# One exp over 1024 columns and a VectorE row sum for the score pair that TensorE masks, in the first batch of a two-layer graph network

## The chip, the cores and the metric

The kernel runs on one core of a Trainium2 chip. The core has five engines with a queue each, all working in parallel: TensorE (PE; its weight loads are listed apart as PEld), VectorE (DVE), ScalarE (ACT), GpSimd (POOL) and SyncE (SP), which here only issues DMAs. They share SBUF; TensorE writes its results to PSUM, from where VectorE and ScalarE read them. The metric is the device time of one execution in microseconds (us). Lower is better.

## The reference

Sixteen graphs of 1024 nodes with 256 features each go through two layers. Cut to what matters:

```
# layer 0, for each graph b: h is a relu of a layer norm of x
normed = layer_norm(h, gamma1, beta1)              # 8 heads of 32 columns; q = k = v
scores = einsum('bhqd,bhkd->bhqk', qkv, qkv) / sqrt(32)
masked = where(adj > 0, scores, -inf)
attn   = softmax(masked, axis=-1)                  # exp, and a sum over the keys
h      = h + einsum('bhqk,bhkd->bhqd', attn, qkv)
x      = x + h + gelu(layer_norm(h) @ W1 + b1) @ W2 + b2
# layer 1: a second attention over the same graph, with leaky relu, softmax and elu
```

The scores are symmetric, since queries and keys are the same, and so is the mask of these inputs. A sum over one axis therefore equals a sum over the other.

## The kernel before

The work of one graph (a "batch" b, 0 to 15) is split into streams: the attention of layer 0 (`attention`), its preparation (`prologue`: layer norms, values `va`, keys `kT`), the masks (`turn_masks`, `compare_masks`), and everything after the attention (`rest`: the two-layer perceptron and all of layer 1). The streams run as Python generators that are merged by a planned place in time; the attention of batch b + 1 is laid between the matmuls of the rest of batch b. Some instructions are put off by a planned number of microseconds (`defer`). What results is one fixed order of instructions for each engine, and at the end of `fast_path` a loop ties every instruction to the one before it on its engine, so that the order written is the order run.

The attention of a batch goes by units (qh, g, kt): a half of the queries (512), a group of four heads, and a tile of 128 keys. The first batch has 2 x 2 x 8 = 32 units, and nothing of a `rest` to lie between them. A unit does the following:

- `scores` (L978): TensorE multiplies keys by queries for four heads (L994) into two PSUM tiles of 128 x 2 x 512, `sc0` for heads 0 and 1 (pair 0) and `sc1` for heads 2 and 3 (pair 1). There is one buffer of each, so the next unit's matmuls into `sc0` wait until this unit's `sc0` has been read.
- The mask is a tile of 0 and of a large negative number. In the first batch (`by_pe = 2 if b == 0 else 0`, L984) TensorE adds it to pair 0 itself, by a matmul with the identity ahead of the scores (L988, its matmuls are listed under the helper's line L574). Pair 1 gets it from VectorE (L1007), which writes the masked scores to an SBUF tile `e`. In all later batches VectorE does this for both pairs.
- ScalarE takes the exponential, one head of 512 columns at a time, and adds up each row as it goes, into a column of a tile `sums`. This is the nested function `weights` (L1011); an exp with such a sum shows as two instructions, ACTIVATE and ACTIVATION_READ_ACCUMULATOR:

```
nc.scalar.activation(
    e[:, j], masked[:, j], AF.Exp, scale=SCALE,
    accum_out=sums[kt // TPH, g][:, n, kt % TPH, qh : qh + 1],
)
```

- For pair 0, `weights` is called inside the loop (L1019), ahead of pair 1's mask addition; for pair 1 it is returned and called by `attention` after the previous unit's `weigh` (L1104: the weights times the values, L1109).
- `invert` (L1125) adds up `sums` over the key halves and takes the reciprocal `rl`; `finish` (L953) turns the result by TensorE (`ptos`, L960), scales it (`ot`, L962) and lets GpSimd add it to `h` (L966).

The engines do other things during the first batch. `setup` multiplies weights (`p_wT`, `p_wb`, `p_wm`, `p_w_a`; copies L678, L694). The prologue of batch 1 takes layer norm statistics on VectorE (`st`, `mv` and `ve`, L741 to L744), their power on GpSimd (`rs`, L746), a factor `nm` on VectorE (L798), a relu on ScalarE (L803), then normalizes, multiplies and adds on GpSimd (`nrm` L750 and L816, `va` L817); TensorE turns `va` (`ptk`, L824) and ScalarE copies it to `kT` (L827). In the first batch's own prologue `nrm` is normalized by VectorE. Mask tiles are converted by VectorE (`mq`, L594), loaded and turned by DMAs of the SP queue (L587, L904), and compared for symmetry by GpSimd and VectorE (`odd` L919, `uneven` L926). At its end `rest` of batch 0 begins: `prepare` (statistics `st_c`), `y` (GpSimd), its turn `pty` (L1275), `yT` (VectorE, L1279), `ph` (TensorE).

Of the kernel before, what the change touches and what calls it, by code (L numbers as in the profile page):

```python
# [14 lines left out]
AF = mybir.ActivationFunctionType  # L15
ALU = mybir.AluOpType
# [479 lines left out]
def fast_path(  # L496
# [28 lines left out]
    nc = tc.nc  # L525
# [10 lines left out]
    TPH = QW // P  # L536
# [3 lines left out]
    SCALE = 1.0 / math.sqrt(HD)  # L540
# [28 lines left out]
    def matmul(out, lhsT, rhs, start=True, stop=True):  # L569
        if not quarters[0]:  # L570
            nc.tensor.matmul(out, lhsT, rhs, start=start, stop=stop)  # L571
            return
        for c in range(0, P, HD):
            nc.tensor.matmul(out[c : c + HD], lhsT[:, c : c + HD], rhs, start=start, stop=stop)  # L574
# [393 lines left out]
    def attention(b, st):  # L968
        va, kT = st["va"], st["kT"]
        mirrored = b > 0  # L970
        sums = {}
# [6 lines left out]
        def scores(qh, g, kt):  # L978
            qs = slice(qh * QW, (qh + 1) * QW)
            sc = [  # L980
                psc.tile([P, 2, QW], F32, tag=f"sc{i}", name=f"s_{b}_{g}_{qh}_{kt}_{i}") for i in range(2)
            ]

            by_pe = 2 if b == 0 else 0  # L984
            if by_pe:
                for j in range(by_pe):
                    matmul(
                        sc[j // 2][:, j % 2, :], ident8, st[qh][:, kt // 2, :, kt % 2], start=True, stop=False  # L988
                    )
                clock[0] += 0.45  # L990
            for j in range(GH):
                r = slice(j * HD, (j + 1) * HD)
                for c in range(0, P, P // 2):
                    nc.tensor.matmul(  # L994
                        sc[j // 2][c : c + P // 2, j % 2, :],
                        kT[r, g, kt * P + c : kt * P + c + P // 2],
                        kT[r, g, qs],
                        start=j >= by_pe,
                        stop=True,
                    )  # L1000
            mb = st[qh][:, kt // 2, :, kt % 2].unsqueeze(1).to_broadcast([P, 2, QW])
            es = []
            for i in range(2):
                e = ep.tile([P, 2, QW], F32, tag="e", name=f"e_{b}_{g}_{qh}_{kt}_{i}")
                masked = sc[i]
                if 2 * i >= by_pe:
                    nc.vector.tensor_tensor(e, masked, mb, op=ALU.add)  # L1007
                    masked = e
                es.append(e)

                def weights(e=e, masked=masked, i=i):  # L1011
                    for j in range(2):
                        n = 2 * i + j
                        nc.scalar.activation(  # L1014
                            e[:, j], masked[:, j], AF.Exp, scale=SCALE,
                            accum_out=sums[kt // TPH, g][:, n, kt % TPH, qh : qh + 1],
                        )

                if i == 0:  # L1019
                    weights()  # L1020
            return es, weights


# [126 lines left out]
        for n, u in enumerate(units):  # L1150
            qh, g, kt = u
            make_turns()
            es, rest_of_weights = scores(*u)
            go_on()
            rest_of_weights()
            first = n == 0 or units[n - 1][:2] != u[:2]
# [488 lines left out]
    while any(p is not None for p in places):  # L1645
        i = min((p, i) for i, p in enumerate(places) if p is not None)[1]
# [72 lines left out]
```

## Time and profile before

| what | value |
|---|---|
| median of three runs | 3445.18 us (3441.09 to 3447.68) |
| the profiled execution | 3447.03 us, its span 3445.2 us |
| TensorE busy over the span | 3250.0 us, 94% |
| VectorE | 2669.7 us, 77% |
| ScalarE | 1987.4 us, 58% |
| GpSimd | 1856.5 us, 54% |
| first exp of the first batch | starts at 23.64 us |
| the last unit's mask addition (unit 32) | starts at 142.19 us |
| L1014, first batch's pair 0 (`e<-s`): 64 exps | 590 ns each, and 64 accumulator reads of 198 ns |
| L1014, all others (`e<-e`): 1504 exps | 619 ns each, and 1504 reads of 187 ns |
| L1007, mask addition, 752 times | 1218 ns each |

How to read it: the profile is one execution, seen by the hardware. Instructions are grouped by line, engine, operation and tile. The idle time before an instruction is given with what ended it. Busy shares are averages over stages that have different limits; the first batch is about 4% of the span.

### The profile page before, as it was taken

What the parts mean: (1) busy time and instruction counts of PE and PEld (TensorE: products, weight loads), DVE (VectorE), ACT (ScalarE), POOL (GpSimd) and SP (SyncE); (2) the same over time, 40 slices, a digit from 0 to 9 for tenths busy, and PEclk for the clock granted to TensorE, in tenths of its full rate; (3) what the DMA queues carried; (4) which work ended last, traced back from release to release, by engine and by line L of the source; (5) the groups of instructions that cost most, each with busy time, mean ns of one, the idle gap of its engine ahead of it and who ended that gap; (6) DMA issues with size and microseconds to landing.
All of it is one profiled execution on the core that took longest, in us unless ns stands there. A gap on an engine that the chain in (4) does not pass through costs nothing. (4 is left out here: it accounts for less than half of the span.)

```text
span 3445.2 us, 114688 instructions
## 1 busy us (share of the span) xinstructions
PE 3250.0 (94%) x48866; PEld 1597.5 (46%) x48866; DVE 2669.7 (77%) x4889; ACT 1987.4 (58%) x4808; POOL 1856.5 (54%) x2006
## 2 busy tenths in 40 slices
PE   6899999999999999999999999999999999999998
PEld 2244444444444444444444444444444444444477
DVE  5678787887878778787887887878788787877744
ACT  6765755647456474655646556575564745646542
POOL 4664663645656465563656737466364565635230
PEclk9999999999999999999999999999999999999999
DMA  5255455464554544545454555545546455554510
GB/s 134 50 123 145 104 122 125 112 159 102 128 120 116 144 112 122 129 114 143 112 133 112 122 139 119 140 106 125 125 112 159 100 131 118 121 142 102 128 38 14
DMA packets 741159, 404.81 MB, mean 118 GB/s; under 512 B 173217, under 2 KB 699937, under 8 KB 740641
## 3 DMA queue, kind: packets, MB, share of 16 engines
q1 hardware_dynamic: 740352, 397.14, 47.7%
q8 instruction: 386, 6.32, 0.8%
q14 instruction: 133, 1.08, 0.1%
q10 hardware_dynamic: 288, 0.26, 0.0%
HBM read 233.97 MB, written 146.54 MB: 110 GB/s over the span
## 5 line engine op out<-in xcount | busy, mean ns | idle before, releaser
L1014 ACT ACTIVATE e<-e 128x512 f32<-128x512 f32 x1504 | 929.3, 619 | 829.5 <-DVE e L1007 827.4
L1007 DVE TENSOR_TENSOR e<-s,mk 128x1024 f32<-128x1024 f32 x752 | 885.9, 1218 | 219.2 <-PE s L994 212.4
L574 PE MATMUL ph<-yT,w 128*32 128x256 f32 x7808 | 445.7, 379 | 23.5 <-DVE yT L1279 15.9
L574 PE MATMUL lg<-fT,uT 128*32 128x256 f32 x7680 | 455.7, 381 | 0.0
L994 PE MATMUL s<-kT 32*64 32x512 f32 x6272 | 451.3, 627 | 1.2 <-DVE e L1007 1.2
L574 PE MATMUL pa<-gw,e 128*32 128x258 f32 x7584 | 446.4, 380 | 0.1
L574 PE MATMUL po<-w,hid 128*32 128x256 f32 x7680 | 442.6, 379 | 0.0
L1109 PE MATMUL o<-e,va 128*32 128x512 f32 x3136 | 432.8, 619 | 1.4 <-ACT e L1014 1.4
L574 PEld LDWEIGHTS ph<-yT,w 128*32 128x32 f32 x7808 | 250.6, 110 | 226.8 <-DVE yT L1279 32.3
L574 PEld LDWEIGHTS po<-w,hid 128*32 128x32 f32 x7680 | 249.9, 110 | 203.0 <-issue 48.8
L574 PEld LDWEIGHTS lg<-fT,uT 128*32 128x32 f32 x7680 | 249.2, 110 | 195.3 <-issue 22.5
L574 PEld LDWEIGHTS pa<-gw,e 128*32 128x32 f32 x7584 | 247.5, 110 | 185.3 <-issue 26.2
L966 POOL TENSOR_TENSOR h<-h,ot 128x512 f32<-128x512 f32 x64 | 84.4, 1319 | 455.7 <-DVE ot L962 455.7
L1030 DVE STREAM_TRANSPOSE x<-e 128x1024 f32<-128x1024 f32 x240 | 296.2, 1239 | 42.3 <-ACT e L1014 40.8
L1043 POOL TENSOR_TENSOR part<-part,x 128x512 f32<-128x512 f32 x240 | 316.7, 1320 | 18.8
L1397 DVE SCALAR_TENSOR_TENSOR e<-lg,gw,mk 128x256 f32<-128x256 f32 x512 | 223.0, 476 | 112.0 <-PE lg L574 100.7
L1014 ACT ACTIVATION_READ_ACCUMULATOR e<-e 128x1 f32 x1504 | 281.5, 187 | 0.0
L1403 ACT ACTIVATE e<-e,shift 128x512 f32<-128x512 f32 x256 | 183.1, 716 | 158.4 <-DVE e L1402 150.5
L1303 ACT ACTIVATE hid<-ph,b1c 128x256 f32<-128x256 f32 x512 | 202.8, 466 | 83.4 <-PE ph L574 63.9
L1043 POOL TENSOR_TENSOR part<-x 128x512 f32<-128x512 f32 x120 | 155.4, 1295 | 176.2 <-DVE x L1030 114.7
L919 POOL TENSOR_TENSOR odd<-mk,mq 128x512 bf16<-128x512 fp8e5 x192 | 234.0, 1226 | 18.1 <-DVE uneven L926 15.6
L746 POOL TENSOR_TENSOR rs_c<-ve_c,mhalf 128x2 f32<-128x2 f32 x64 | 45.6, 713 | 359.4 <-DVE ve_c L744 323.9
(144 smaller groups left out, 4613.7 us busy)
## 6 DMA issues: line engine op xcount, KB each, us to landing
blocks<-x SPq DMA_DIRECT2D x480, 256.0 KB, 4.7
em<-blocks SPq DMA_DIRECT2D x240, 512.0 KB, 5.0
adj<-in_adj_dram SPq DMA_DIRECT2D x248, 256.0 KB, 3.9
h<-in_x_dram SPq DMA_DIRECT2D x64, 256.0 KB, 4.1
xb<-in_x_dram SPq DMA_DIRECT2D x128, 128.0 KB, 3.3
out_dram<-z SPq DMA_DIRECT2D x128, 128.0 KB, 3.9
rows<-row SPq DMA_DIRECT2D x120, 32.0 KB, 2.3
gather<-rows SPq DMA_DIRECT2D x120, 32.0 KB, 3.4
```

What stands on the lines that cost most here:

```text
L574: nc.tensor.matmul(out[c : c + HD], lhsT[:, c : c + HD], rhs, start=start, stop=stop)
L919: nc.gpsimd.tensor_tensor(odd.rearrange("p (u v x) -> p u v x", u=2, v=2), key.rearrange("p (u v x) -> p u v x", u=2, v=2), query.rearrang ...
L966: nc.gpsimd.tensor_add(ho, ho, ot.rearrange("p t j d -> p t (j d)"))
L994: nc.tensor.matmul(sc[j // 2][c : c + P // 2, j % 2, :], kT[r, g, kt * P + c : kt * P + c + P // 2], kT[r, g, qs], start=j >= by_pe, stop= ...
L1007: nc.vector.tensor_tensor(e, masked, mb, op=ALU.add)
L1014: nc.scalar.activation(e[:, j], masked[:, j], AF.Exp, scale=SCALE, accum_out=sums[kt // TPH, g][:, n, kt % TPH, qh : qh + 1],)
L1030: nc.vector.transpose(x[:, :, 2 * i : 2 * i + 2, :].rearrange("p c h j -> p h c j"), es[i].rearrange("p h (c i) -> p h c i", i=HD),)
L1043: add = lambda out, p, q: nc.gpsimd.tensor_tensor(out, p, q, op=ALU.add)
L1109: nc.tensor.matmul(o[j * HD : (j + 1) * HD, :], va[:, kt, (g * GH + j) * HD : (g * GH + j + 1) * HD], es[j // 2][:, j % 2, :], start=first ...
L1303: nc.scalar.activation(hid[:, f0 + i, :], ph[:, i, :], AF.Identity, bias=b1c[:, f0 + i : f0 + i + 1])
L1397: nc.vector.scalar_tensor_tensor(e[:, j, :], lg[:, j, :], gw[:, kt, D : D + 1], st[c // 2][:, kt // 2, qs, kt % 2], op0=ALU.add, op1=ALU.add,)
L1403: ready = defer(2.5, lambda: nc.scalar.activation(e, e, AF.Exp, bias=shift))
```

## The change

For the pair whose mask TensorE adds (pair 0, in the first batch only), `weights` issues a single exp over both heads, 1024 columns, without a row sum. VectorE then adds up each head's 512 results by a `tensor_reduce` over `e`, into the two columns of `sums`. The call for pair 0 is moved behind the loop, so that both instructions come after pair 1's mask addition on VectorE's queue. Nothing changes for pair 1, or for the later batches.

```diff
                 def weights(e=e, masked=masked, i=i):
+                    if 2 * i < by_pe:
+                        nc.scalar.activation(e, masked, AF.Exp, scale=SCALE)
+                        nc.vector.tensor_reduce(
+                            sums[kt // TPH, g][:, 2 * i : 2 * i + 2, kt % TPH, qh : qh + 1].rearrange(
+                                "p h o -> p (h o)"
+                            ),
+                            e, axis=mybir.AxisListType.X, op=ALU.add,
+                        )
+                        return
                     for j in range(2):
                         n = 2 * i + j
                         nc.scalar.activation(
...
-                if i == 0:
+                if i == 0 and by_pe == 0:
                     weights()
+                elif i == 0:
+                    first = weights
+            if by_pe:
+                first()
             return es, weights
```

## The prediction

> **What bounds the kernel now.** The change touches only the first batch (`by_pe` is 2 for b = 0 and 0 for all others), so I read the page for the whole and then only the first 146 us. The page gives PE 94% of the span. From 146 us on, where the next stage joins the first attention's successor, PE has almost no gaps, so a delay of the first batch's end is carried to the end of the kernel unchanged. The question is thus when the 32 units of the first batch are done. First the waits of 20 to 146 us (who waited for whom, us in total, times, longest):
>
> ```profile
> PE s L574 <- ACT e L1014: 10.0, 18, 1.4
> ...
> PE ptk L824 <- POOL va L817: 6.4, 3, 2.9
> ```
>
> TensorE waits for the first pair's exps before it can write the next unit's masks, 18 times; and three times for GpSimd, which prepares the next batch's values. Then the timeline of one quiet unit (start, duration, engine; the bracket is the idle time before it):
>
> ```profile
> 42.25 0.60 ACT L1014 ACTIVATE e<-s 128x512 f32<-128x512 f32 x1 [0.39 <-PE s L994]
> 42.34 1.22 DVE L1007 TENSOR_TENSOR e<-s,mk 128x1024 f32<-128x1024 f32 x1 [1.52 <-ACT e L1014]
> ...
> 43.32 0.20 ACT L1014 ACTIVATION_READ_ACCUMULATOR e<-s 128x1 f32 x1
> ...
> 43.57 0.61 PE L574 MATMUL s<-mk,ident 128*32 128x512 fp8e5 x8 [0.42 <-ACT e L1014]
> ...
> 43.60 0.63 ACT L1014 ACTIVATE e<-e 128x512 f32<-128x512 f32 x1
> ```
>
> The reader is to see a ring: exps of pair 0 from 42.25 to 43.52, which free `sc0`; masks from 43.57; scores from 44.12; the next exp at 45.33. A turn takes 3.08 us, of which PE idles 0.42 and VectorE (DVE) about 1.5. Such slack is not everywhere. In other units DVE goes from one add to the next without a gap:
>
> ```profile
> 68.41 1.23 DVE L1007 TENSOR_TENSOR e<-s,mk 128x1024 f32<-128x1024 f32 x1 [3.04 <-PE s L994]
> 69.55 0.75 DVE L594 TENSOR_SCALAR mq<-adj 128x512 fp8e5<-128x512 int32 x2
> 70.22 0.42 DVE L741 BATCH_NORM_STATS2 st_b<-h 128x6 f32<-128x256 f32 x1
> ...
> 71.50 1.22 DVE L1007 TENSOR_TENSOR e<-s,mk 128x1024 f32<-128x1024 f32 x1
> ```
>
> Last the busy times by stretch (length, then PE, PEld, DVE, ACT, POOL):
>
> ```profile
> 58.95:83.90 24.95, 20.01 (x312) 5.83 (x312) 17.09 (x44) 21.50 (x66) 8.87 (x12) 1.00 0.43 112
> 83.90:113.50 29.60, 22.59 (x236) 6.13 (x220) 16.59 (x28) 20.98 (x65) 28.63 (x30) 0.96 0.00 1
> ```
>
> DVE is two thirds busy in the first; GpSimd has 28.63 of 29.60 us in the second and is the bound there. Its run starts with one DVE result, and PE stands at its end:
>
> ```profile
> 83.90 0.69 POOL L746 TENSOR_TENSOR rs_a<-ve_a,mhalf 128x2 f32<-128x2 f32 x1 [2.36 <-DVE ve_a L744]
> ```
> ```profile
> 112.67 0.90 PE L824 MATMUL ptk<-ident,va 128*128 128x128 f32 x3 [2.48 <-POOL va L817]
> ```
>
> [...] The trace agrees: the copies from PSUM of 257 and 512 columns take 353 and 564 ns, 0.827 a column. [...] The two rows below agree: 391 ns for 386 columns more, 1.01 a column. [...]
>
> ```profile
> L728 DVE TENSOR_REDUCE seen<-sq 128x1 f32<-128x512 f32 x1 | 0.7, 675 | 0.0
> ...
> L1230 DVE TENSOR_REDUCE seen<-good 128x1 f32<-128x126 f32 x1 | 0.3, 284 | 0.0
> ```
>
> **Prices.** Exp over 1024 columns from PSUM: 590 ns for 512 (row L1014 e<-s) + 512 x 0.83 = 1.02 us. It frees `sc0` 1.02 us after its start, where the two exps and their accumulator reads took 1.27: 0.25 less a turn. On ACT's queue the two took 1.14 us from start to start of what follows (75.04 to 76.18 us), the one takes about 0.92. Bounds: 0.96 and 1.10. The reduce: [...] 1.21 us, like the add of as many columns (1.22), whose follower starts 1.14 after it; so 1.13 us more of DVE's queue a unit. Bounds: [...] 1.35 (two reduces of 512).
>
> **Part by part.** Removed: 64 exps of 512 and their 64 accumulator reads on ACT. Added: 32 exps and 32 reduces, 32 x 1.13 = 36 us of DVE. Moved: the exp is issued after the add, on another engine, so ACT's order stays. The reduce waits for its exp; behind it in DVE's queue stand the layer norm statistics (GpSimd's `rs` waits for them), `nm` (ACT's relu L803 waits for it), the mask conversions (SP's DMAs wait for these) and the next add. The exp usually ends before the add does (42.25 + 1.02 against 43.48), so that wait costs nothing unless ACT is late. No DMA is added, and PE's list is the same.
>
> Now the units in order, by the lag of the new against the old (minus is earlier):
> - Units 1 to 5 (23.7 to 39.3 us). The reduce stands ahead of the statistics on which GpSimd's `rs_b`, the `nrm` of DVE and so the next add depend (25.4 to 33.15 us, GpSimd without a gap from 27.5). All move by 1.13: **+1.13**.
> - Units 5 to 11. Four turns have PE waiting for ACT: 4 x -0.25. The two others are full of other PE work (`p_wT`, `p_wb`): 0. DVE needs 1.14 + 1.13 + 0.34 = 2.61 us of the new 2.83 in the quiet ones. Lag **+0.13**; the add of unit 10 is at +0.25 for its mask conversion.
> - Unit 11 to 12: DVE 1.14 + 1.13 + 1.27 of statistics = 3.54 against 3.09. Add at +0.59. Unit 13 starts behind exp, relu and the copy of `wm` (63.4 to 66.0), all behind that add: +0.6.
> - 13 to 14: 1.14 + 1.13 + 0.67 + 1.28 = 4.22 against 3.09: +1.7. 14 to 15: 3.62 against 3.07: +2.3. 15 to 16: DVE has nothing else, back to +1.45. 16 to 17: 3.61 against 3.07: +2.0.
> - Unit 17: relu L803 waits for `nm`, now at 83.2 for 80.6; the exp behind it starts at 84.36, the reduce at 84.36 + 1.05 = 85.41; then 1.13 and 1.26 of statistics: `ve_a` at 87.80 for 83.65. Lag **+4.15**.
> - GpSimd's run of 83.9 to 112.6 starts by so much later and has no room; DVE's and PE's lags in it, up to 5, are covered by it. At 113.5: +4.15.
> - Units 25 to 32: two quiet turns give -0.5. At 128.75 the mask conversions come behind a reduce and `rl` behind both: +0.3. The DMAs of the masks, released by those conversions, land later by 4.8 (before: conversions waiting for them at 132.93, 133.63 and 138.06), and adds 30 and 31 with them: +4.8. The last reduce stands beside the wait for `pty`.
>
> Sum: **+4.8 us** at 146 us, and to the end. The profiled execution took 3447.03 us (span 3445.2), so 3451.8 against it; it lay 1.85 above the median of 3445.18, so I predict **3450.0 us**. The bounds of the reduce move the sum by about -1 and +2 (13 units where DVE is the bound), those of the exp by about 0.5, my reading of which wait ends last by 3 to 4.
>
> **Rivals.**
> - *B, the second pair's exps wait for the reduce.* Reduce and exps write columns of the same tile `sums`. If that is taken as a conflict, ACT's second pair starts after the reduce, 2.5 us after the first exp instead of 1.35; a turn is 2.5 + 1.25 = 3.75 us for 3.08. That is some 0.9 worse than the forecast in the six turns bound by ACT or PE before 60 us, 1.1 at each of units 12, 14 and 16, and 3 after 113 us: about +15, 3460. Against it: the columns are disjoint (heads 0, 1 and 2, 3). It decides as soon as the wait exists. This is the case on the other side.
> - *C, DVE's backlog outlasts the first batch.* Its add of unit 32 is at +5.3; if `yT` at 145.34, on which `ph` waits, comes behind more of such work, PE loses another 3 to 5: 3454. For it: after 200 us DVE is 90% busy and more.
> - *D, hidden.* The statistics ahead of 83.9 are not the last arrival; the run of GpSimd starts as before: about 0, 3445. Against it: GpSimd idled 2.36 us for exactly that.
> - *E, the ring decides.* All 18 waits of PE shrink by 0.25: -4.5, 3440.7. The most that 32 units could give is 8 us.
>
> **How the numbers follow.** 0.2%, 6.9 us, is about what a measurement of this kernel can tell from no change. Forecast 0.52, own range 3445 to 3455 (0.34 of it within 0.2%, 0.18 above), B 0.12, C 0.14, D 0.13, E 0.09 (0.05 beyond 0.2%, and 0.01 of D). Slower 0.18 + 0.12 + 0.14 = 0.44, same 0.50, faster 0.06. The range from 3443 to 3460 leaves E's side and B's upper side out.
>
> **What would show it.** L1014 e<-s 32 times near 1.02 us, the reduce 32 times near 1.21, quiet turns of 2.83 us, `ve_a` near 88 and `va` near 117 us. B would show as ACT's e<-e waiting for the reduce. Wrong I am if GpSimd's run starts near 84, or if PE makes up the lag after 146 us.

## The result, and the profile after

The changed kernel takes 3457.8 us (median of 8 runs, 3452.47 to 3464.07) and the kernel before, measured beside it, 3445.1 us (8 runs, 3440.16 to 3450.47). The ratio is 1.0036, with a 95% interval from 1.0025 to 1.0046: by the ratio 12.4 us slower, with 8.6 to 15.8 as the interval. The profiled execution took 3458.48 us, its span 3456.6 us. The forecast was 3450.0 with a range to 3460: the side is right, and the loss is more than twice the 4.8 us of the forecast.

I read the trace in the order of the prediction. First the two new groups, from the list of groups by shape, 20 to 160 us of the changed kernel (busy us and mean ns of one; then the idle time before them):

```profile
L1014 DVE TENSOR_REDUCE sum<-e 128x2 f32<-128x1024 f32 x32 | 38.8, 1211 | 2.6 <-ACT e L1013 2.6
L1013 ACT ACTIVATE e<-s 128x1024 f32<-128x1024 f32 x32 | 32.6, 1019 | 13.4 <-PE s L994 13.3
```

Both prices are the predicted ones, 1.21 and 1.02 us. A quiet turn is the predicted one too (2.83 us for 3.08): ScalarE's timeline of the changed kernel has the wide exp 2.84 us after the last, and nothing stands between the wide exp and pair 1's but the mask addition.

```profile
43.24 1.02 ACT L1013 ACTIVATE e<-s 128x1024 f32<-128x1024 f32 x1 [0.20 <-PE s L994]
44.54 0.63 ACT L1023 ACTIVATE e<-e 128x512 f32<-128x512 f32 x1 [0.27 <-DVE e L1007]
...
46.08 1.03 ACT L1013 ACTIVATE e<-s 128x1024 f32<-128x1024 f32 x1 [0.20 <-PE s L994]
```

So the single prices hold, and the sum does not. The waits of the changed kernel, 20 to 160 us, say where (us in total, times, longest):

```profile
PE s L574 <- ACT e L1013: 9.0, 15, 2.5
...
PE ptk L824 <- POOL va L817: 6.9, 3, 3.3
POOL odd L919 <- DVE uneven L926: 6.7, 3, 3.3
```

TensorE's waits for the exps went from 10.0 us in 18 waits to 9.0 us in 15; that is all that is left here of the shorter turns. The third line is the news: GpSimd waits three times for VectorE's `uneven`, where before it did so once, for 2.37 us at 40.90. Two of the three lie in its full run, of which I had said that it covers VectorE's lag. GpSimd's timeline of the changed kernel:

```profile
89.48 0.69 POOL L746 TENSOR_TENSOR rs_a<-ve_a,mhalf 128x2 f32<-128x2 f32 x1 [3.92 <-DVE ve_a L744]
...
98.88 1.15 POOL L919 TENSOR_TENSOR odd<-mk,mq 128x512 bf16<-128x512 fp8e5 x1
102.49 1.16 POOL L919 TENSOR_TENSOR odd<-mk,mq 128x512 bf16<-128x512 fp8e5 x1 [2.46 <-DVE uneven L926]
...
114.78 1.16 POOL L919 TENSOR_TENSOR odd<-mk,mq 128x512 bf16<-128x512 fp8e5 x1 [0.98 <-DVE uneven L926]
...
121.18 0.72 POOL L817 TENSOR_TENSOR va<-nrm,be 128x256 f32<-128x256 f32 x1
```

The run begins 5.58 us late (83.90 before), loses 2.46 and 0.98 us inside, and its last `va` starts 9.29 us late (111.89 before). TensorE stands at its end, as before, and the lag goes on from there (TensorE's timeline of the changed kernel, then of the kernel before: the masks of unit 25):

```profile
121.96 0.90 PE L824 MATMUL ptk<-ident,va 128*128 128x128 f32 x3 [2.65 <-POOL va L817]
122.79 1.04 PE L574 MATMUL s<-mk,ident 128*32 128x512 fp8e5 x8
```
```profile
113.50 1.04 PE L574 MATMUL s<-mk,ident 128*32 128x512 fp8e5 x8
```

The first scores of the second batch start at 154.75 us for 145.23, +9.52. In the later batches of this profile the lag moves between 7 and 12 us, and at the end of the span it is 11.4. A second profile of the changed kernel has the same lag at the second batch, counted from the first mask addition, and only 2.4 us at the end of its span, so a single profile does not tell what is left at the end; the two timed ratios, 1.0036 and 1.0037, do. Why GpSimd had to wait is in VectorE's timeline of the changed kernel around the first of the two waits:

```profile
98.18 1.21 DVE L1007 TENSOR_TENSOR e<-s,mk 128x1024 f32<-128x1024 f32 x1
100.86 1.22 DVE L1014 TENSOR_REDUCE sum<-e 128x2 f32<-128x1024 f32 x1 [1.47 <-ACT e L1013]
102.00 1.93 DVE L926 TENSOR_TENSOR uneven<-uneven,odd 128x256 int32<-128x256 int32 x2
```

A comparison goes through two buffers of `odd`: GpSimd writes one, VectorE adds it to `uneven` and so frees it. From 98.88 to 100.03 GpSimd filled the second; the addition that would free the first stood behind the new reduce, and the reduce waited 1.47 us for its exp. The third comparison began only after 102.00.

### The profile page after: what moved, and what is told of

The parts are those of the page before. It is cut to its first block, busy times and chain, and to the rows that moved or that the text cites. A ratio compares the mean times of both kernels' runs of the same rounds, so it can differ in the third digit from the quotient of the medians.

```text
span 3456.6 us, 114602 instructions
## 1 busy us (share of the span) xinstructions
PE 3259.9 (94%) x48866; PEld 1598.3 (46%) x48866; DVE 2704.1 (78%) x4921; ACT 1985.6 (57%) x4712; POOL 1861.4 (54%) x2006
## 3 DMA queue, kind: packets, MB, share of 16 engines
q14 instruction: 132, 1.08, 0.1%
## 5 line engine op out<-in xcount | busy, mean ns | idle before, releaser
L1007 DVE TENSOR_TENSOR e<-s,mk 128x1024 f32<-128x1024 f32 x752 | 885.6, 1218 | 199.9 <-PE s L994 194.8
L994 PE MATMUL s<-kT 32*64 32x512 f32 x6272 | 458.7, 633 | 3.4 <-DVE e L1007 3.4
```

The lines of the kernel that those rows point to most:

```text
L994: nc.tensor.matmul(sc[j // 2][c : c + P // 2, j % 2, :], kT[r, g, kt * P + c : kt * P + c + P // 2], kT[r, g, qs], start=j >= by_pe, stop= ...
```

## The experiments

Marks are counted from the first mask addition of VectorE, since that start itself lies between 23.70 and 24.66 us from profile to profile. They are the addition of unit 11, the start of GpSimd's full run (`rs_a`), the masks of unit 25 on TensorE (the end of that run), and the first scores of batch 2 (the end of the first batch). Ratios are against the kernel before, timed beside each on the same chip.

| kernel | unit 11 | run | unit 25 | batch 2 | median us | ratio, 95% interval |
|---|---|---|---|---|---|---|
| before | 35.30 | 60.17 | 89.77 | 121.50 | 3445.1 | 1 |
| changed | 36.52 | 65.78 | 99.09 | 131.05 | 3457.8 | 1.0036 [1.0025, 1.0046] |
| a_again (the changed kernel once more) | 36.58 | 65.79 | 99.09 | 131.06 | 3451.94 | 1.0037 [1.0021, 1.0052] |
| e1_short | 34.38 | 59.50 | 89.47 | 120.23 | 3443.65 | 0.9991 [0.9982, 1.0000] |
| e7_reduce_only | 39.33 | 70.00 | 102.35 | 133.13 | 3460.03 | 1.0043 [1.0028, 1.0057] |
| e2_odd_own | 38.91 | 68.77 | 98.28 | 130.65 | 3453.57 | 1.0023 [1.0015, 1.0031] |
| e2_again | 38.37 | 67.70 | 97.23 | 129.01 | 3453.94 | 1.0020 [1.0011, 1.0029] |
| e4_late_reduce | 36.13 | 63.40 | 93.91 | 123.66 | 3452.19 | 1.0024 [1.0017, 1.0031] |
| e3_adj_own | 35.64 | 64.61 | 96.68 | 127.81 | 3450.17 | 1.0033 [1.0020, 1.0047] |
| e5_before_late_compare | 35.31 | 60.17 | 82.61 | 117.22 | 3440.99 | 0.9995 [0.9984, 1.0006] |
| e6_after_late_compare | 36.27 | 65.24 | 87.65 | 122.85 | 3447.83 | 1.0013 [1.0003, 1.0024] |
| e9_late_both | 36.01 | 62.85 | 85.91 | 121.03 | 3447.06 | 1.0005 [0.9997, 1.0012] |
| e8_quiet_late_compare | 34.51 | 60.40 | 82.90 | 118.07 | 3442.22 | 0.9994 [0.9984, 1.0004] |
| e10_before_late_adj | 35.32 | 60.21 | 82.67 | 116.32 | 3439.5 | 0.9986 [0.9974, 0.9997] |

The changed kernel was profiled twice: its marks repeat within 0.06 us, while the span differs by 9.0 us. The marks thus show where time goes in the first batch, and the ratios what is left of it at the end. But a mark is of one execution: TensorE runs at half clock (0.50 granted) in short stretches, whose place differs between executions (last section) and which moved marks by some 1.5 us; in the two profiles of the changed kernel those that matter happen to fall alike.

My theory was that the loss is a matter of VectorE's queue: 1.13 us a unit, ahead of the statistics that start GpSimd's run and of the `uneven` that frees its buffers. The rivals were that the reduce costs by *waiting* for the exp, that it costs as a *load* wherever it stands, that the wide *exp* is what hurts, and, for the part before 60 us, the *landing* of mask transfers.

**A short instruction in the reduce's place.** It waits for the same exp and writes the same columns; the row sum of the first pair is left out.

```diff
-nc.vector.tensor_reduce(sums[...], e, axis=mybir.AxisListType.X, op=ALU.add)
+nc.vector.tensor_scalar(sums[...], e[:, :, 0], 0.0, 1.0, op0=ALU.mult, op1=ALU.add)
```

> In place of the row sum of the first pair VectorE writes ones, by an instruction over one column of each head that still waits for the exp (the row sum of that pair is left out). The order of all queues and the wait for the exp stay; VectorE's extra 1.13 us a unit falls to some 0.15. Theory 'queue' (the length of the reduce in VectorE's queue costs the time): GpSimd's run starts near 82 to 84 us (changed kernel 89.5, kernel before 83.9), the masks of unit 25 start near 111.5 to 114 us (122.8 and 113.5), the kernel takes 0 to 4 us less than before. Rival 'wait' (VectorE standing in wait for the exp costs it): the masks of unit 25 start at 116 us or later, and the kernel takes 3 to 7 us more than before.

The loss is gone: 0.9991. The wait is still there, 2.6 us in 4 waits from 20 to 160 us (2.6 in 3 in the changed kernel), as VectorE's timeline of this kernel shows for one of them:

```profile
82.05 0.17 DVE L1014 TENSOR_SCALAR sum<-e 128x2 f32<-128x2 f32 x1 [0.93 <-ACT e L1013]
...
83.39 0.17 DVE L744 TENSOR_SCALAR ve_a<-mv_a 128x2 f32<-128x2 f32 x1
```

The rival of the wait falls: with as much waiting and a short instruction nothing is lost, so what delays is the time that the reduce takes. (A wait that comes with the lag, as the 1.47 us at 100.86 in the changed kernel, still adds to what stands behind it.) The run also shows what the wide exp is worth at most. With 32 shorter turns and almost no price on VectorE, batch 2 starts 1.27 us earlier; unit 11 had gained 0.92, the run's start 0.67, unit 25 only 0.30. The mark at the end of GpSimd's run keeps little of the ring's first gain, and only the last units, behind that run, bring some again.

**The reduce alone.** The kernel before keeps its two exps, and VectorE also does the reduce, into a tile that nobody reads: extra work, nothing left out.

```diff
                 if i == 0:
                     weights()
+            if by_pe:
+                nc.vector.tensor_reduce(twice, es[0], axis=mybir.AxisListType.X, op=ALU.add)
             return es, weights
```

> The kernel before, with its two exps and their row sums, plus a reduce of the same columns on VectorE at the place of the changed kernel, into a tile that nobody reads. Theory 'queue': the loss is that of the changed kernel or 0 to 2 us more, since the shorter ring of TensorE and ScalarE (0.25 us a turn) is not there: masks of unit 25 at 122.5 to 125 us. Rival 'exp' (part of the loss is from the single exp of 1024 columns): the loss is clearly smaller, masks at 120 us or earlier.

1.0043: the whole loss of the changed kernel, and batch 2 at +11.6 us for +9.6. The rival of the exp falls: the reduce alone is enough for the loss. The mark of unit 25 is later than expected (127.01 on the trace's own clock). The first mask addition is 0.96 us later in this profile, and TensorE ran at half clock in units 4 and 5 (8 matmuls of 2.32 us at 37.77, for 1.40 at 36.73 in the changed kernel), by which unit 5's addition is 1.67 us behind the changed kernel's; more on this below.

**GpSimd's two buffers.** In the second half's comparisons of the first batch each `odd` gets room of its own, in a tile that is free at that time; the reduce stays.

```diff
-odd = smallp.tile([P, QW], BF16, tag="odd", bufs=2, ...)
+if (b, qh) == (0, 1):
+    if half == i == 0:
+        own = midp.tile([P, 2 * TPH, QW], BF16, tag="mid2", name="odd_own")
+    odd = own[:, half * TPH + i]
```

> The changed kernel, but the eight mask comparisons of the first batch's second half write to eight places of their own instead of two in turn. Theory 'two buffers' (GpSimd stood 2.46 and 0.98 us because VectorE, delayed by the reduces, gave the comparison buffers back late): both waits go, the masks of unit 25 start near 119.3 us instead of 122.8, and the kernel takes some 3.5 us less than the changed one, 6 to 9 us more than before. Rival [...] (VectorE's added work slows GpSimd's own instructions): GpSimd's instructions get longer, the masks stay at 122 us or later.

GpSimd's timeline of the second profile of this kernel: the two comparisons at 101.05 follow each other without a gap, and `nrm` follows them.

```profile
101.05 2.27 POOL L924 TENSOR_TENSOR odd_own<-mk,mq 128x512 bf16<-128x512 fp8e5 x2
103.30 1.40 POOL L750 TENSOR_SCALAR nrm<-h,mv_b,rs_b 128x256 f32<-128x256 f32 x1
```

From `rs_a` to the last `va` the run takes 27.9 us, as before (27.99), against 31.70 in the changed kernel. That settles the handshake: 3.8 us. The rival that GpSimd's own instructions got slower falls: the eight comparisons of the run average 1.16 us here and before and 1.18 in the changed kernel, 0.2 us in all. But the run began 2 to 3 us later than in the changed kernel, which I had not expected, and unit 25 came only 0.8 us earlier instead of 3.5. To see whether this was an accident of one profile I ran it again.

> The kernel with own places for the comparisons once more. Its first profile had GpSimd's run free of waits (27.9 us from its first power to the last values, as in the kernel before, against 31.7), but the run began 3.3 us later than in the changed kernel, behind slow TensorE work at 37 to 40 us. If that was an accident of the run, the run of GpSimd now begins at 89.5 to 90.5 us and the masks of unit 25 come at 119 to 120 us. If it belongs to the kernel, both come as in its first profile, 92.8 and 122.3 us, and the timed gain over the changed kernel is small.

The second profile does not tell: the run began 1.9 us late again, but TensorE also had the same stretch of half speed again (its timeline in the second profile; the same 8 matmuls take 1.40 us at 36.73 in the changed kernel, the turn of `va` 0.65):

```profile
37.10 2.26 PE L1127 MATMUL o<-e,va 128*32 128x512 f32 x8
39.29 1.12 PE L824 MATMUL ptk<-ident,va 128*128 128x128 f32 x4
```

By this stretch unit 5's addition is some 1.5 us late, and that this comes from where the clock's steps lay in these two executions, not from the edit, is my estimate from the last section; no run shows it. The ratios, 1.0023 and 1.0020, are 4 to 5 us better than the changed kernel's, which is about the handshake's size; the intervals overlap, and the marks at batch 2 gained only 0.4 and 2.0 us.

**The reduce behind the statistics.** The reduce of a unit is held back and issued at the top of the next unit, behind the layer norm statistics and ahead of the next mask addition. Same work, other place.

```diff
-nc.vector.tensor_reduce(sums[...], e, axis=mybir.AxisListType.X, op=ALU.add)
+late.append(lambda: nc.vector.tensor_reduce(sums[...], e, axis=mybir.AxisListType.X, op=ALU.add))
...
 qh, g, kt = u
+if late:
+    late.pop()()
 make_turns()
```

> The changed kernel, but each reduce is issued a unit later, right ahead of the next unit's mask addition: behind the statistics, the relu factor and the comparison, and with its exp long done. VectorE's work is the same. Theory 'queue', in the form that it counts what stands behind the reduce: GpSimd's run starts near 87.3 us instead of 89.5, its waits for the comparison fall below 1 us, the masks of unit 25 start at 117 to 118.5 us instead of 122.8; some 4 us of the loss come back. Rival 'load' (VectorE is simply short of time, whatever the order): the masks stay within 1 us of 122.8.

VectorE's timeline of this kernel now has `ve_a` first and the reduce behind it; in the changed kernel `ve_a` started at 89.23:

```profile
87.04 0.17 DVE L744 TENSOR_SCALAR ve_a<-mv_a 128x2 f32<-128x2 f32 x1
87.12 1.22 DVE L1015 TENSOR_REDUCE sum<-e 128x2 f32<-128x1024 f32 x1
```

The run starts at 87.29 us, unit 25's masks at 117.80, as expected, and the two waits of GpSimd shrink to 0.36 us each. In the trace 7.4 of 9.6 us at batch 2 are back with all 32 reduces still done, so in the trace it is mostly the place that costs, and little the load as such. The timed runs give back less, about 4 us (1.0024 for 1.0036), and leave 8.3 us that this does not explain.

**The masks' landing.** The mask tiles of the first batch get eight places of their own for the two that rotate.

```diff
-a = adjp.tile([P, QW], I32, tag="adj", ...)
+if b == 0:
+    k = (t - TPH) * 2 + c // QW
+    if k % 4 == 0:
+        room[0] = midp.tile([P, 4, QW], I32, tag=f"mid{k // 4}", ...)
+    a = room[0][:, k % 4]
```

> The changed kernel, but the mask tiles that the first batch loads for its second half have eight places of their own instead of two in turn, so that their DMAs don't wait for the conversions on VectorE. Theory 'landing' (the conversions, moved back by the reduces, released the next DMAs later, and VectorE then stood 0.66 us for a mask at 59.9 us with the mask addition of unit 11 behind it, at 60.2 instead of the predicted 59.2): VectorE no longer waits for a mask between 50 and 75 us, unit 11's addition starts some 0.9 us earlier against unit 10's, GpSimd's run starts near 88.6 us instead of 89.5. Rival: the wait moves into the next unit, and GpSimd's run starts at 89.5 as before.

This is about unit 11. VectorE's timeline of the changed kernel, then of this one:

```profile
59.88 0.43 DVE L594 TENSOR_SCALAR mq<-adj 128x512 fp8e5<-128x512 int32 x1 [0.66 <-DMA adj<-in_adj_dram]
60.22 1.22 DVE L1007 TENSOR_TENSOR e<-s,mk 128x1024 f32<-128x1024 f32 x1
```
```profile
57.89 0.75 DVE L602 TENSOR_SCALAR mq<-adj_own 128x512 fp8e5<-128x512 int32 x2
59.93 1.22 DVE L1015 TENSOR_TENSOR e<-s,mk 128x1024 f32<-128x1024 f32 x1 [1.29 <-PE s L1002]
```

With the transfers early, the addition waits for TensorE's scores again. Unit 11 gains 0.88 us, the run's start 1.2, unit 25 2.4, batch 2 3.2. VectorE has no wait for a mask from 50 to 75 us any more. The landing is real in the trace; the timed ratio of 1.0033 cannot tell it from the changed kernel's.

**Later comparisons.** If GpSimd's full run is the gate, then taking work out of it must help both kernels. The second half's comparisons of the first batch are planned later (the place is in batches), without the change and with it.

```diff
-spread(compare_masks(b, 1, states[b]), 2 * TPH, b + (0.58 if b else 0.52), b + 0.73)
+spread(compare_masks(b, 1, states[b]), 2 * TPH, b + (0.58 if b else 0.74), b + (0.73 if b else 0.82))
```

> The kernel before, with the eight mask comparisons of the first batch's second half planned at 0.74 to 0.82 of the batch instead of 0.52 to 0.73, behind GpSimd's work on the next batch's values. Theory 'GpSimd's run' (TensorE waits at 113 us for a run of GpSimd that is full, 8 us of it comparisons): the run ends near 105 us instead of 112.6, the masks of unit 25 start at 105 to 108 us instead of 113.5, and the kernel takes 4 to 8 us less than before. Rival (TensorE's and ScalarE's ring sets the time, GpSimd's end only looks like it): masks at 112 us or later, no change of the time.

> The changed kernel with the comparisons moved in the same way. If GpSimd's full run was what passed the delay on, VectorE's queue takes its place as the bound: masks of unit 25 at 109 to 112 us, 4 to 6 us later than in the kernel before with the same move, and the kernel takes about as long as before (-2 to +3 us). If the exp's shorter ring comes out once GpSimd is out of the way, the changed kernel with the move is as fast as the kernel before with the move, or faster.

Without the change unit 25 comes 7.2 us earlier and batch 2 4.3, but the 4 to 8 us expected of the whole kernel did not show: the timed ratio of 0.9995 doesn't resolve a gain. With the change unit 25 is 5.0 us later than without and batch 2 5.6, and the kernel is 4.5 us slower than before where -2 to +3 was expected. TensorE no longer waits for a `va` there in either kernel, and the 5 us are there already at the start of the run (65.24 for 60.17): with GpSimd's run shortened, the delay that VectorE's queue brought up to then stays. GpSimd's timeline of the second kernel also shows it waiting inside the run, not for `uneven` but for statistics:

```profile
104.78 0.71 POOL L746 TENSOR_TENSOR rs_b<-ve_b,mhalf 128x2 f32<-128x2 f32 x1 [1.15 <-DVE ve_b L744]
```

So no placing of GpSimd's work tried here lets the ring's gain come out. Late reduce and late comparisons together:

> The changed kernel with both moves: the reduce a unit later, right ahead of the next addition, and the comparisons behind GpSimd's values. Theory 'queue': what the late reduce gave (2.2 us at the start of GpSimd's run) adds to what the late comparison gave. Second batch's scores, counted from the first mask addition, at 119 to 121 us (changed kernel 131.05, before 121.5, before with late comparison 117.2); time within 3 us of the kernel before. If VectorE's load alone counts, the same as the changed kernel with late comparison, 122.8.

Batch 2 starts at 121.03, just past the edge of what was expected. The late reduce brings the run's start forward by 2.4 us, as it did alone, but batch 2 only by 1.8 us (121.03 for 122.85), where alone it gave 7.4. So the two do not add in full: most of what the late reduce gave lay in and behind GpSimd's run, which the late comparisons shorten anyway. At 1.0005 this is level with the kernel before; in the trace it is 3.8 us behind the late comparisons alone.

**The change only where VectorE is idle.** Late comparisons, and the changed form in eight quiet units only.

```diff
+room = qh * 16 + g * 8 + kt in (4, 5, 6, 7, 9, 24, 25, 26)
...
-if 2 * i < by_pe:
+if 2 * i < by_pe and room:
```

> The kernel before with late comparisons, and the change's single exp and reduce only in eight units where VectorE has room (5 to 8, 10, 25 to 27). Theory 'queue': the ring's 0.25 us a turn comes out where nothing of VectorE's stands behind the reduce: 1 to 2 us less than the kernel before with late comparisons, second batch's scores at 115.5 to 116.5 us from the first addition (117.2 there), the kernel 2 to 6 us faster than before. Rival (the form with the reduce is never worth it): 117 us or more.

Batch 2 at 118.07 misses the expectation: it is 0.85 later than with late comparisons alone. Until unit 11 it was 0.80 ahead. Then TensorE fell to half clock, 0.50 granted from 68 to 70 us (its timeline, this kernel first, then late comparisons alone):

```profile
66.82 1.77 PE L995 MATMUL s<-kT 32*64 32x512 f32 x16
68.51 1.94 PE L1123 MATMUL o<-e,va 128*32 128x512 f32 x8
```
```profile
67.66 1.11 PE L994 MATMUL s<-kT 32*64 32x512 f32 x16
68.71 1.06 PE L1109 MATMUL o<-e,va 128*32 128x512 f32 x8
```

These two lines lose 0.66 and 0.88 us, more than the gain. Another execution may lack that stretch (last section), and 0.9994 timed is level with 0.9995 for the late comparisons alone, so what the quiet units are worth stays open.

**The two best placings without the change**: late comparisons and the masks' own places.

> The kernel before (two exps with row sums on ScalarE), with the comparisons behind GpSimd's values and with own places for the first batch's mask tiles: the two waits that the runs showed, without the change. Expected: second batch's scores at 115 to 117.2 us from the first addition (121.5 before, 117.2 with the late comparisons alone), 4 to 7 us less than before, a ratio near 0.9985. Rival: VectorE's waits for masks were covered in the kernel before, and nothing is added to the late comparisons: 117.2 us, ratio 0.9990.

0.9986: 3439.5 us, the only one of thirteen intervals that lies wholly below 1, by a thin margin. Batch 2 starts at 116.32, 5.2 us early, which is 0.15% of the time and agrees.

## Why the prediction was right, and where its size was wrong

The mechanism was the forecast one: VectorE pays 1.13 us a unit, the delay reaches the start of GpSimd's run, TensorE stands at its end, and by the timed ratios it is not made up later. That 3457.8 lies inside the range is in part luck: the range went up to 3460 for other cases, B's among them, and the forecast's own sum ended at 3450.0. By the steps, as lags of the changed against the kernel before:

| step | predicted | measured |
|---|---|---|
| unit 5's addition | +1.13 | +1.17 |
| unit 11's addition | +0.13 | **+1.18** |
| unit 14's addition | +1.7 | +2.95 |
| `ve_a` of unit 17 | +4.15 | +5.58 |
| masks of unit 25 | +4.15 | **+9.29** |
| batch 2 | +4.8 | +9.52 |

- *Units 1 to 5*, the *prices* and the *quiet turn* are right. So is 13 to 14 (4.21 us for 4.22). The forecast's two rows, 675 ns for 512 columns and 1.01 for each one more, make 1192 ns for the reduce, and the add of as many columns took 1218; measured are 1211. The 1 us less in the forecast, for a shorter reduce, was my estimate.
- *"Units 5 to 11 ... Lag +0.13"* is the first wrong term. The four shorter turns were there, but the mask conversion of unit 9 was late (54.39 for 52.81), its place came free late, and the conversion that waited for the next mask started 1.87 us later (59.88 for 58.01), right ahead of unit 11's addition. I had followed such a release for units 29 to 31 and not for this one. The masks' own places gave 0.88 of these 1.05 us back. Another 0.38 us came on the way to `ve_a`; 0.28 of it is one small VectorE instruction, `ve_b` at 84.25, with 0.45 us for the 0.17 of the same one in the kernel before (at 80.52).
- *"GpSimd's run ... has no room; DVE's and PE's lags in it ... are covered by it. At 113.5: +4.15"* is the second, and the larger: 3.71 us. That GpSimd is busy without a gap meant that its inputs were in time, not that they would stay so when VectorE is later. It hands VectorE its results through two buffers, so VectorE's lag beyond the slack of two buffers stops it. The 2.46 + 0.98 us are 3.44 of the 3.71. Shown by the separate buffers (run back at 27.9 us) and the late reduce (waits of 0.36). Not all of that lag is reduces: VectorE's addition at 89.97 had stood 0.57 us for scores that TensorE wrote at half clock (0.50 granted from 86.47 to 89.88), so up to that much of the first wait may be the clock's.
- *Units 25 to 32* were to add 0.65 and added 0.23. The three together are 1.43 + 3.71 - 0.42 = 4.72, the gap between 4.8 and 9.52.
- *The reduce beside GpSimd's work*: all 32 take 1204 to 1223 ns, those in GpSimd's run too. `uneven`, on the same engine, does not stay so even: 418 ns as median and up to 1414 in the changed kernel, 416 and 1367 before, the long ones in GpSimd's run. What makes them long was not shown.
- *B* is absent: ScalarE's second pair waits for the mask addition alone. *D* falls with `rs_a` at 89.48. *E* falls twice: the ring is worth 1.27 us, not 4.5, when VectorE pays almost nothing. *C* gave a time near the measured one, 3454, by another mechanism: VectorE's backlog did reach another engine, but inside the first batch, and nothing was lost at `yT`.

What stays open: the timed difference, 12.4 us, is 2.9 above the trace's 9.5, within its interval. For the late reduce the gap is wider, 8.3 us timed for 2.2 in the trace, and for the masks' own places too, 11.4 for 6.3; no run explains it. The mean granted clock goes with it in part. In the 48 runs of the kernel before on that chip, the mean time falls from 3450.5 us at 0.987 to 3440.7 at 0.991, some 2.5 us for 0.001; the late reduce averages 0.9879 and the kernel before 0.9890. A trace is also one execution, with its own stretches of half clock, while the timed figure is of many. Whether the later VectorE lowers the clock in later batches, or this is scatter, was not tried.

## What to carry to other kernels

A reduction taken off an engine that has slack, and put in another's queue, costs by its place there more than by its share of that engine's busy time: list what stands behind it and who waits for that. Where two engines hand results over through two buffers, follow the handshake in both directions; an engine that is busy without a gap can be stopped by the one that frees its buffers. And when a gain frees a ring for 0.25 us a turn, look for the next gate first: here it was GpSimd's run, and in the traces moving work out of that run brought batch 2 forward by 4.3 us, where the change without its price brought 1.3. The timed ratios do not tell these two apart.

## What the runs showed of the hardware

TensorE drops to half clock for short stretches in the first batch. In the clock records such a stretch has a granted clock of 0.50, it lasts 3.41 or 6.83 us there, and the starts lie whole steps of 3.41 us apart: in the kernel before at 111.20 and 141.92 us, 9 steps apart; in the changed kernel at 69.40, 86.47, 120.60 and 151.32 us, which are 5, 10 and 9 steps apart; in the second profile with the `odd` buffers apart at 37.39, 71.52, 102.24 and 119.31, which are 10, 9 and 5 apart. Where the steps lie differs between the profiles: counted from the first mask addition a step begins at 1.33 and 1.41 us in the two profiles of the changed kernel, at 2.97 and 3.07 in the two with the buffers apart, at 3.23 with the reduce alone and at 0.75 with the short instruction.

The clearest stretch follows TensorE's wait at the end of GpSimd's run. These are two steps of the kernel before (start and end, length, busy us of TensorE, its weight loads, VectorE, ScalarE, GpSimd, then the granted clock):

```profile
107.79:111.20 3.41, 0.33 (x1) 0.14 (x1) 0.63 (x2) 1.33 (x4) 3.17 (x5) 1.00 0.00 0
111.20:114.61 3.41, 1.94 (x19) 0.77 (x27) 0.00 (x0) 0.59 (x1) 2.45 (x3) 0.50 0.00 0
```

Half clock also follows steps that are far from idle. Here are two steps with the `odd` buffers apart, then the same place of the changed kernel, where TensorE is busy for as long but the steps lie elsewhere, and the clock stays full from 28 to 42 us:

```profile
33.98:37.39 3.41, 2.33 (x20) 0.49 (x22) 3.23 (x5) 1.33 (x5) 2.73 (x5) 1.00 0.11 41
37.39:40.80 3.41, 3.41 (x20) 1.03 (x14) 2.45 (x3) 2.97 (x8) 2.91 (x3) 0.50 0.00 0
```
```profile
33.51:36.92 3.41, 2.32 (x23) 0.56 (x22) 3.13 (x5) 1.22 (x4) 2.72 (x5) 1.00 0.06 22
```

What brings the half clock about the runs do not show. The longest gap of TensorE in the step from 33.98 was 1.08 us. With the change in quiet units, 2.14 busy us in the step from 63.74 were followed by half clock; in the kernel before, 2.14 in the step from 63.42 were not.

So a stretch of half clock in one profile is not a property of the kernel alone. It cost both profiles with the buffers apart some 1.5 us by unit 5, and the one with the change in quiet units more than its gain. It need not cost anything either: the second profile of the changed kernel has 6.83 us of half clock from 100.98 that the first lacks, inside GpSimd's run, and unit 25 starts at the same mark, since TensorE waits for that run anyway.
